# Spreading four half exponentials over the change of blocks, and moving one TensorE piece, in a graph attention kernel

## The chip, the cores and the metric

The kernel runs on one core of one Trainium2 chip, in one launch. The metric is device time in microseconds (us), lower is better; the number is the median of three runs. A core has five engines that run side by side and meet only at semaphores: TensorE (PE in the profile, its weight loads PEld), VectorE (DVE), ScalarE (ACT), GpSimd (POOL) and SyncE (SP), which issues transfers. Each engine takes its instructions strictly in the order in which they are written.

## What is computed

Two layers of a graph network over 3327 nodes with 128 features, dense adjacency matrix. Cut to what matters:

```python
# layer 0: graph attention with a mask, then residual and layer norm
e = leaky_relu(A * s + A * r.T);  att = softmax(where(A > 0, e, NEG), axis=1)
x = layernorm(x + att @ H)
# layer 1: 128 attention "heads" d, each with 8 features h, n = m = 3327
a = einsum('dnh,dmh->dnm', q, k) * scale + adj + adj
a = softmax(a, axis=2)
out = einsum('dnm,dmh->dnh', a, v).reshape(n, 1024) @ Wo.T
x = layernorm(x + out)
```

Nearly all of the time goes into layer 1: 128 x 3327 x 3327 exponentials, and the two products around them.

## The kernel before, in words

**Blocks, chunks and rounds.** Heads are taken four at a time: 32 groups `g`. The 3327 columns `n` are cut into 7 blocks of 476. For one group and one block (224 such blocks in all), the 3327 keys are walked in 26 chunks of 128 (one has 127), numbered 0 to 25. A chunk's tile `e4` holds 4 heads x 476 columns for 128 keys; a *half* is two of the four heads, 952 numbers a partition. The chunks are cut into *stretches* of three: (0,1,2), (3,4,5) and so on to (21,22,23); the last stretch has two chunks only, (24,25).

The adjacency enters in two ways. In the first chunk of each stretch (0, 3, ... 24; I call it a **product chunk**; `times` in the code) ScalarE takes the exponential of the scores straight from PSUM (L992), and GpSimd multiplies by a factor, 1 or e² (L993). In the other chunks (**sum chunks**) VectorE adds the adjacency to the scores (L995), and ScalarE takes the exponential afterwards, in place (L828, in the function `exp_late`). The exponential of a whole sum chunk is one instruction of 1904 numbers a partition.

The work is laid out in 26 *rounds* a block. Each round handles two halves. In a stretch i, i+1, i+2 the three rounds are: half of i and half of i+1; the other half of i and of i+1; both halves of i+2. The last stretch has just rounds 24 and 25. So in rounds 24, 25 and, in the next block, 0 and 1, four rounds in a row have a half of a product chunk; elsewhere every third round has none.

**The order in a round.** The loop writes, round by round: the score matmuls of the two halves (L135; four matmuls on four row groups of the array); then zero to two *pieces* of TensorE side work (`work_tensor`); then for each half L992 and L993, or L995; then `exp_late()`; then the products with the values (`products`, L800) of the chunk whose turn was four rounds ago (LAG = 4); then side work of VectorE and GpSimd (`work`). The side work is layer 0 of the rows to come and the output projection of the rows that are done: per piece one matmul such as L311, L365 or L479, and on VectorE small instructions such as L304, L284 or L374 and L377. `lane` says in which rounds there is room for it. A piece is taken only where the next unit of the side work is one for TensorE; a projection (L365), for one, is followed by a VectorE unit (L374, L377) which must be done before the next one.

**Buffers that make engines wait.** Scores of a product half go to one PSUM buffer (`pe`, one copy): the next product half's scores wait until L992 has read it. Scores of a sum half go to `pd` with two copies: they wait for the L995 of two halves ago. The products of a block pile up in one PSUM bank `av`; after the last one (written at the end of round 3 of the next block) VectorE copies it out (L809), and the first product of the next block (in round 4) waits for that copy.

**What is late.** `exp_late()` runs what the round before put on the list `late`. So chunk 23, finished in round 23, gets its whole exponential in round 24; the two halves of chunk 25 get theirs in rounds 25 and 0. In units of half a chunk ScalarE is given, in rounds 24, 25, 0, 1, 2, 3: 3, 2, 2, 1, 2, 3 units (its own L992 counted). `lane("p", n)` gives one TensorE piece in rounds 4, 7, ... 22 and 25, and two in round 24.

Of the kernel before, what the change touches and what calls it, by code (L numbers as in the profile page):

```python
# [47 lines left out]
def kernel(  # L48
# [31 lines left out]
    NT = -(-N // P)  # L80
# [7 lines left out]
    HG = 4  # L88
    NG = D // HG
# [44 lines left out]
    def scores(dst, k4, q4, i, r, j, nb, stop=True):  # L134
        nc.tensor.matmul(  # L135
            dst,
            k4[32 * j : 32 * j + H4, i::NT],
            q4[32 * j : 32 * j + H4, :nb],
            start=True,
            stop=stop,  # L140
        )


    def special():
        with ExitStack() as sx, tc.manual_schedule(engines=ALL):
# [86 lines left out]
            def tick(all_=False):  # L232
                for p in pend:
                    p[0] -= 1
                while pend and (all_ or pend[0][0] <= 0):
                    pend.pop(0)[1]()
# [471 lines left out]
            for m, st_ in enumerate(stretch):  # L708
                starts[len(rounds)] = m
                if len(st_) > 1:  # L710
                    i = st_[0]
# [5 lines left out]
            NR = len(rounds)  # L717
# [4 lines left out]
            def open_group(g):  # L722

                k4 = kp.tile([P, N], F32R, name="k4b")
                v4 = kp.tile([P, HG, VW], F32, name="v4b")
                nc.gpsimd.memset(v4[:, :, REST * H1 :], 0.0)

                def keys(j, engine=nc.sync):
                    engine.dma_start(
                        k4[32 * j : 32 * j + H4, :].bitcast(F32),  # L730
                        _ap(kT, (g * HG + j) * N, [[G, 2 * H], [0, 2], [1, N]]),
                    )

                def values(p0, p1, k, engine=nc.sync):
                    engine.dma_start(
                        v4[p0:p1, :, : k * H1],
                        _ap(vd, (g * HG * N + p0 * NT) * H1, [[NT * H1, p1 - p0], [N * H1, HG], [1, k * H1]]),
                    )

                parts = [lambda j=j, **kw: keys(j, **kw) for j in range(HG)]  # L740
                for p0, p1, k in [c + (NT,) for c in _cut(FP)] + [(FP, P, REST)]:
                    parts.append(lambda c=(p0, p1, k), **kw: values(*c, **kw))
                return k4, v4, parts
# [19 lines left out]
            def want_adj(n):  # L763

                if n >= len(stretches):
                    return
                g, b, m = stretches[n]
                a = adjs[n] = ap_.tile([P, 3, WB], F32, name="at")
                n0 = blocks[b][0]
                cs = stretch[m]  # L770
                if n >= RAW and cs[0] in times:
                    nc.sync.dma_start(a[:, 0, :], ftd[b][m])
                    cs = cs[1:]
                z = where[cs[0]]
                there = sum(i < REST for i in cs)
                parts = [(0, P, there)]
                if there < len(cs):
                    parts = [c + (len(cs),) for c in _cut(FP)] + [(FP, P, there)]
                for p0, p1, k in parts:
                    if k:  # L780
                        nc.sync.dma_start(
                            a[p0:p1, z : z + k, :],
                            _ap(adjT, (p0 * NT + cs[0]) * N + n0, [[NT * N, p1 - p0], [N, k], [1, WB]]),
                        )
# [34 lines left out]
            waiting = []  # L819


            late = []

            def exp_late():
                while late:
                    s, i, h0, h1 = late.pop(0)
                    e = s.e[i][: kr[i], h0:h1, :]
                    nc.scalar.activation(e, e, AF.Exp, scale=2.0)  # L828

# [5 lines left out]
            total = NBLK * NR  # L835
# [8 lines left out]
            def lane(kind, n):  # L844
                middle = n % 3 == 1 and 4 <= n < NR - 2
                if kind == "p":
                    return (1, 2)[n == NR - 2] if middle or n >= NR - 2 else 0
                return int(middle or n == 0 or n >= NR - 2)

            made = [layer0(t) for t in range(1, NT)]  # L850
# [3 lines left out]
            for n, (_, m, a) in enumerate(made):  # L854

                later = []
                for u in a:
                    if u[0] == "r":

                        at = max((k for k, v in enumerate(aside) if v[0] == "n"), default=0)  # L860
# [70 lines left out]
            def finish_to(mark, now):  # L931
                while mark not in marks:
                    row = "main" if head("main", -1 if now is None else now, True) else "aside"
                    if head(row, -1 if now is None else now, True) is None:
                        break
                    run(row, -1)
                    tick(True)
# [14 lines left out]
            for g in range(NG):  # L952
                k4, v4, _ = group
                for b in range(NBLK):
                    s = Block()
                    s.g, s.b, s.q4, s.k4, s.v4, s.left, s.e, added = g, b, queries[0], k4, v4, NT, {}, {}
                    for n, rnd in enumerate(rounds):
                        at = b * NR + n
                        if n in starts:
                            m = (g * NBLK + b) * NST + starts[n]  # L960
                            want_adj(m + AHEAD)
                            a = adjs[m]
                        tick()
                        if g + 1 < NG:
                            if at == total - OPEN:
                                finish_to(("rows", reads[g + 1]), None)
                                tick(True)
                                group = open_group(g + 1)
                            for k, f in enumerate(group[2]):
                                if at >= total - OPEN and at == total - OPEN + OPEN * k // len(group[2]):  # L970
                                    f()
                        if n == NR // 2 and (b + 1 < NBLK or g + 1 < NG):
                            queries = open_queries(g, b + 1) if b + 1 < NBLK else open_queries(g + 1, 0)
                        for j in range(HG):
                            if n == NR // 2 + j * (NR > 12) and (b + 1 < NBLK or g + 1 < NG):
                                queries[1](j)
                        sc = []
                        for i, h in rnd:
                            sc.append((pe if i in times else pd).tile([P, 2, 512], F32, name="scb"))
                            for t in range(2):  # L980
                                scores(sc[-1][: kr[i], t, :WB], s.k4, s.q4, i, kr[i], 2 * h + t, WB)
                        work_tensor(g * total + at, n)
                        for (i, h), z in zip(rnd, sc):
                            r = kr[i]
                            if i not in s.e:
                                s.e[i] = sp.tile([P, HG, WB], F32, name="e4")
                                added[i] = 0
                            eh = s.e[i][:r, 2 * h : 2 * h + 2, :]
                            added[i] += 1
                            ah = a[:r, where[i], :].unsqueeze(1).to_broadcast([r, 2, WB])  # L990
                            if i in times:
                                nc.scalar.activation(eh, z[:r, :, :WB], AF.Exp, scale=2.0)  # L992
                                nc.gpsimd.tensor_tensor(eh, eh, ah, op=ALU.mult)  # L993
                            else:
                                nc.vector.tensor_tensor(eh, z[:r, :, :WB], ah, op=ALU.add)  # L995
                        exp_late()
                        for i, h in rnd:
                            if i in times:
                                continue
                            if NT % 3 == 2 and i == NT - 1:  # L1000
                                late.append((s, i, 2 * h, 2 * h + 2))
                            elif added[i] == 2 and (s, i, 0, HG) not in late:
                                late.append((s, i, 0, HG))
                        if n + 1 in starts or n + 1 == NR:
                            del adjs[m]
                            make_factor(m + 1)
                        waiting.append((s, order[n]))
                        while len(waiting) > LAG:
                            products(*waiting.pop(0))
                        work(g * total + at, n)  # L1010
            exp_late()
            while waiting:
                products(*waiting.pop(0))
            tick(True)
# [378 lines left out]
```

## Time and profile before

| | us |
|---|---|
| median of three runs | 10442.8 (10442.0 to 10449.3) |
| the profiled execution's own time | 10444.2 |
| its span, first to last instruction | 10442.3 |
| L993, GpSimd's multiplications, 4032 of them | 8971.6 busy, 2.234 each |
| L995, VectorE's additions, 7616 | 8418.5 busy, 1.145 each |
| L800, products with the values, 46592 | 5874.8 busy, 0.576 each, four at a time |
| L135, score matmuls, 23296 | 4348.8 busy, 0.592 each, four at a time |
| L809, copy of a block's products, 224 | 144.3 busy, 0.644 each |

How to read it: a matmul's duration is that of one instruction, but four of them run side by side on separate parts of the array, so busy time is far below count times duration. The busy share is an average; whether an engine holds up the rest is read from what the others wait for.

Two stretches of the trace, both with one piece a stretch, in the view of busy time by window: 4875.00 to 4880.26 us, three rounds in the middle of a block, has PE busy 5.26 us, ACT 5.18, DVE 4.91, POOL 4.41 out of 5.26. Across a change of blocks, in the timeline of TensorE, the score matmuls of rounds 24, 25, 0, 1, 2, 3, 4, 5 start at 4847.95, 4850.28, 4852.39, 4854.13, 4855.60, 4857.48, 4859.20 and 4861.11 us. The rounds are therefore 2.33, 2.11, 1.74, 1.47, 1.88, 1.72 and 1.91 us long.

### The profile page before, as it was taken

Reading aid. Unit: us, or ns where it says so; the run is one execution under the profiler, and the core shown is the slowest. Engines: PE = TensorE matmul, PEld = TensorE weight load, DVE = VectorE, ACT = ScalarE, POOL = GpSimd, SP = SyncE. Lnnn points to the kernel's source line nnn. Section 1 sums busy time; section 2 is a strip of 40 time slices with the busy share of each in tenths; the row PEclk is TensorE's granted clock in tenths of the full one; section 3 lists DMA queues with packets and bytes.
Section 4 is the critical chain, followed back from the end, with each engine's and each line's share of the span. In section 5 each row is a group of like instructions: output and inputs, shape, how many; then the busy total and the mean of one; then the engine's idle time right before and its main releaser. Section 6 shows DMA issues by size and latency. Waiting matters only on the chain.

```text
span 10442.3 us, 195151 instructions
## 1 busy us (share of the span) xinstructions
PE 10174.5 (97%) x73245; PEld 3799.9 (36%) x73245; DVE 9401.7 (90%) x12247; ACT 10077.8 (97%) x8087; POOL 9229.0 (88%) x4395
## 2 busy tenths in 40 slices
PE   7999999999999999999999999999999999999998
PEld 3333333333333333333333333333333333333333
DVE  6999999999989999989999998999999899998887
ACT  6999999999999999999999999999999999999998
POOL 6988898889888889888889888888888888888887
PEclk8999999999999999999999999999999999999999
DMA  6655555555555555555555555555555555555554
GB/s 174 200 169 165 167 166 171 166 169 159 173 159 169 166 161 167 173 163 171 153 169 169 166 175 164 157 163 175 171 164 164 159 169 172 165 155 165 162 156 123
DMA packets 1176730, 1728.91 MB, mean 166 GB/s; under 512 B 121852, under 2 KB 1164381, under 8 KB 1171547
## 3 DMA queue, kind: packets, MB, share of 16 engines
q1 hardware_dynamic: 1174410, 1714.80, 55.0%
q8 instruction: 576, 9.44, 0.4%
q14 instruction: 383, 3.14, 0.1%
q10 hardware_dynamic: 1361, 1.53, 0.1%
HBM read 1611.92 MB, written 103.95 MB: 164 GB/s over the span
## 4 chain that ended last, share of the span: by engine, by line
PE 79%; ACT 13%; DVE 3%; issue 2%; POOL 2%; DMA 1%; SPq 0%; DVEq 0%; ACTq 0%; POOLq 0%
PE av L800 40%; PE scb L135 33%; ACT e L992 7%; ACT e L828 6%; PE bank L311 2%; PE bank L365 2%; DVE e L995 2%; POOL e L993 1%; PE bank L479 1%; DVE o L809 0%; DMA at<-in_adjT_dram 0%; POOL at L790 0%; PE bank L460 0%; DMA trow<-td 0%; DVE lo L377 0%
## 5 line engine op out<-in xcount | busy, mean ns | idle before, releaser
L993 POOL TENSOR_TENSOR e<-e,at 128x952 f32<-128x952 f32 x4032 | 8971.6, 2234 | 1099.2 <-ACT e L992 911.1
L995 DVE TENSOR_TENSOR e<-scb,at 128x952 f32<-128x952 f32 (+1 forms) x7616 | 8418.5, 1145 | 914.4 <-PE scb L135 651.8
L828 ACT ACTIVATE e<-e 128x1904 f32<-128x1904 f32 (+1 forms) x4032 | 6856.9, 1701 | 79.0 <-DVE e L995 77.2
L800 PE MATMUL av<-e,v4b 128*32 128x476 f32 x46592 | 5874.8, 576 | 28.9 <-DVE o L809 19.2
L135 PE MATMUL scb<-q4b,k4b 32*128 32x476 f32 (+1 forms) x23296 | 4348.8, 592 | 180.6 <-ACT e L992 99.0
L135 PEld LDWEIGHTS scb<-q4b,k4b 32*128 32x128 f32 (+1 forms) x23296 | 2390.9, 295 | 5002.8 <-issue 1984.9
L992 ACT ACTIVATE e<-scb 128x952 f32<-128x952 f32 x4032 | 3873.8, 961 | 203.0 <-PE scb L135 103.1
L800 PEld LDWEIGHTS av<-e,v4b 128*32 128x32 f32 x46592 | 919.4, 108 | 1216.6 <-issue 810.6
L311 PE MATMUL bank<-hsb,w 128*128 128x129 f32 (+2 forms) x1300 | 300.7, 321 | 0.0
L304 DVE TENSOR_SCALAR_CACHE_REDUCE dump<-a 128x384 bf16<-128x384 f32 (+2 forms) x468 | 247.4, 529 | 0.6
L284 DVE TENSOR_SCALAR_CACHE_REDUCE w<-trow,er 128x128 f32<-128x128 f32 (+1 forms) x650 | 221.1, 340 | 20.6 <-DMA trow<-td 12.6
L311 PEld LDWEIGHTS bank<-hsb,w 128*128 128x128 f32 (+2 forms) x1300 | 188.6, 188 | 133.5 <-issue 133.5
L295 POOL TENSOR_TENSOR w<-w,a 128x384 f32<-128x384 f32 (+3 forms) x225 | 221.6, 985 | 0.1
L809 DVE COPY o<-av 128x476 f32<-128x476 f32 x224 | 144.3, 644 | 5.5 <-PE av L800 5.5
L377 DVE SCALAR_TENSOR_TENSOR lo<-bank,hi 128x128 fp32r<-128x128 f32 (+1 forms) x400 | 116.7, 292 | 13.9
L374 DVE TENSOR_SCALAR hi<-bank 128x128 fp32r<-128x128 f32 (+1 forms) x400 | 112.5, 281 | 0.0
L365 PE MATMUL bank<-wv,x1T 128*128 128x128 f32 (+1 forms) x400 | 98.2, 328 | 4.8 <-DVE vb L396 4.3
L365 PE MATMUL bank<-wk,x1T 128*128 128x128 f32 (+1 forms) x400 | 97.6, 326 | 3.7 <-DVE lo L377 3.2
L365 PE MATMUL bank<-wq,x1T 128*128 128x128 f32 (+1 forms) x400 | 97.7, 326 | 2.9 <-DVE lo L377 1.9
L479 PE MATMUL bank<-wo,ot 128*128 128x128 f32 (+1 forms) x416 | 95.9, 325 | 0.4 <-DVE ot L469 0.4
L365 PEld LDWEIGHTS bank<-wv,x1T 128*128 128x128 f32 (+1 forms) x400 | 59.8, 188 | 51.4 <-issue 39.9
L365 PEld LDWEIGHTS bank<-wk,x1T 128*128 128x128 f32 (+1 forms) x400 | 59.5, 187 | 50.9 <-issue 40.3
(111 smaller groups left out, 824.9 us busy)
## 6 DMA issues: line engine op xcount, KB each, us to landing
at<-in_adjT_dram SPq DMA_DIRECT2D x1736, 476.0 KB
at<-ftd SPq DMA_DIRECT2D x1953, 238.0 KB
q4b<-qT SPq DMA_DIRECT2D x1788, 29.8 KB
k4b<-kT SPq DMA_DIRECT2D x126, 415.9 KB
at<-in_adjT_dram SPq DMA_DIRECT2D x217, 208.2 KB
at<-in_adjT_dram SPq DMA_DIRECT2D x56, 714.0 KB
a<-in_adjT_dram SPq DMA_DIRECT2D x50, 504.0 KB
ftd<-at SPq DMA_DIRECT2D x63, 238.0 KB
```

The source lines that it names most:

```text
L135: nc.tensor.matmul(dst, k4[32 * j : 32 * j + H4, i::NT], q4[32 * j : 32 * j + H4, :nb], start=True, stop=stop,)
L284: nc.vector.tensor_scalar(w, s["t"][:, :r], e, None, op0=ALU.max, op1=ALU.add, accum_out=spare[:, 0:1])
L295: nc.gpsimd.tensor_tensor(w, w, s["a"][n][:, c0 - i0 : c1 - i0, :r], op=ALU.mult)
L304: nc.vector.tensor_scalar(z, a, float(k), None, op0=ALU.is_equal, op1=ALU.add, accum_out=even[:, t, at : at + 1])
L311: nc.tensor.matmul(s["p"][:r, : D + 1], s["w"][i // CW][: kr[i], i % CW, :r], hsb[: kr[i], i, :], start=(i == 0), stop=(i == NT - 1),)
L365: nc.tensor.matmul(s["b"][:r, :QW], s["xT"][:, :r], w[:, c : c + QW], start=True, stop=True)
L479: nc.tensor.matmul(s["b"][:r, :D], s["ot"][:, h, :r], wo[:, h, :], start=(h == 0), stop=(h == H - 1))
L800: nc.tensor.matmul(s.av[32 * j : 32 * j + 32, :], s.v4[:r, j, i * H1 : i * H1 + 32], e[:r, j, :], start=(s.left == NT - 1), stop=(s.left = ...
L828: nc.scalar.activation(e, e, AF.Exp, scale=2.0)
L992: nc.scalar.activation(eh, z[:r, :, :WB], AF.Exp, scale=2.0)
L993: nc.gpsimd.tensor_tensor(eh, eh, ah, op=ALU.mult)
L995: nc.vector.tensor_tensor(eh, z[:r, :, :WB], ah, op=ALU.add)
```

## The change

The list `late` gets a due round for each entry. A whole sum chunk is due one round after its second half, as before. Chunk 23 (`NT - 3`) is now taken in two halves, due in rounds 24 and 25. Chunk 25 (`NT - 1`) is still in halves, each now due two rounds after its addition, in rounds 0 and 1 of the next block. ScalarE's units in rounds 24, 25, 0, 1, 2, 3 are then 2, 2, 2, 2, 2, 3. In `lane`, round 24 has room for one TensorE piece in place of two, and round 3 for one in place of none.

```diff
-            def exp_late():
-                while late:
-                    s, i, h0, h1 = late.pop(0)
+            def exp_late(now):
+                for item in [x for x in late if x[0] <= now]:
+                    late.remove(item)
+                    _, s, i, h0, h1 = item
                     e = s.e[i][: kr[i], h0:h1, :]
                     nc.scalar.activation(e, e, AF.Exp, scale=2.0)
...
                 if kind == "p":
-                    return (1, 2)[n == NR - 2] if middle or n >= NR - 2 else 0
+                    return int(middle or n == 3 or n >= NR - 2)
...
-                        exp_late()
+                        now = g * total + at
+                        exp_late(now)
                         for i, h in rnd:
                             if i in times:
                                 continue
                             if NT % 3 == 2 and i == NT - 1:
-                                late.append((s, i, 2 * h, 2 * h + 2))
-                            elif added[i] == 2 and (s, i, 0, HG) not in late:
-                                late.append((s, i, 0, HG))
+                                late.append((now + 2, s, i, 2 * h, 2 * h + 2))
+                            elif NT % 3 == 2 and i == NT - 3:
+                                late.append((now + 1 + h, s, i, 2 * h, 2 * h + 2))
+                            elif added[i] == 2 and (now + 1, s, i, 0, HG) not in late:
+                                late.append((now + 1, s, i, 0, HG))
...
-            exp_late()
+            exp_late(NG * total + 2)
```

## The prediction

> **What bounds the kernel now.** I read the page first: engine shares, the chain, the groups.
>
> ```profile
> PE 10174.5 (97%) x73245; PEld 3799.9 (36%) x73245; DVE 9401.7 (90%) x12247; ACT 10077.8 (97%) x8087; POOL 9229.0 (88%) x4395
> ...
> PE 79%; ACT 13%; DVE 3%; issue 2%; POOL 2%; DMA 1%; SPq 0%; DVEq 0%; ACTq 0%; POOLq 0%
> ...
> L828 ACT ACTIVATE e<-e 128x1904 f32<-128x1904 f32 (+1 forms) x4032 | 6856.9, 1701 | 79.0 <-DVE e L995 77.2
> ...
> L992 ACT ACTIVATE e<-scb 128x952 f32<-128x952 f32 x4032 | 3873.8, 961 | 203.0 <-PE scb L135 103.1
> ```
>
> TensorE and ScalarE are both 97% busy, and the chain runs 79% through TensorE, 13% through ScalarE. Neither has more than 3% to give, so the change can only win stalls at the change of blocks. The window view finds no TensorE idle in a middle stretch with a piece (5.26 of 5.26 us); middle stretches without one last 5.07 us in the TensorE timeline. Next I read the timeline at two changes of blocks. Time 0 is from here the start of round 24's scores. First ScalarE, at a change with no TensorE piece (0 = 4940.19):
>
> ```profile
> 4941.75 1.78 ACT L828 ACTIVATE e<-e 128x1904 f32<-128x1904 f32 x1
> 4943.43 0.96 ACT L992 ACTIVATE e<-scb 128x952 f32<-128x952 f32 x1
> 4944.28 1.00 ACT L828 ACTIVATE e<-e 127x952 f32<-127x952 f32 x1
> 4945.21 0.96 ACT L992 ACTIVATE e<-scb 128x952 f32<-128x952 f32 x1
> 4946.07 0.99 ACT L828 ACTIVATE e<-e 127x952 f32<-127x952 f32 x1
> 4946.96 0.96 ACT L992 ACTIVATE e<-scb 128x952 f32<-128x952 f32 x1
> 4948.51 1.79 ACT L828 ACTIVATE e<-e 128x1904 f32<-128x1904 f32 x1 [0.59 <-DVE e L995]
> 4950.36 0.96 ACT L992 ACTIVATE e<-scb 128x952 f32<-128x952 f32 x1
> ```
>
> Chunk 23's whole exponential (1.78) stands ahead of round 25's L992; round 0's scores need that L992's buffer and start at 4944.44. Then ScalarE runs dry (0.59, and again before 4950.36). This is a real stall. Now TensorE at a change with projections in rounds 24 and 25 (0 = 4847.95):
>
> ```profile
> 4854.13 0.60 PE L135 MATMUL scb<-q4b,k4b 32*128 32x476 f32 x4 [0.20 <-ACT e L992]
> 4854.66 1.01 PE L800 MATMUL av<-e,v4b 128*32 128x476 f32 x8
> 4855.60 1.02 PE L135 MATMUL scb<-q4b,k4b 32*128 32x476 f32 x4
> 4856.55 1.00 PE L800 MATMUL av<-e,v4b 127*32 127x476 f32 x8
> 4857.48 0.62 PE L135 MATMUL scb<-q4b,k4b 32*128 32x476 f32 x4
> 4858.04 1.00 PE L800 MATMUL av<-e,v4b 128*32 128x476 f32 x8
> ```
>
> The product of chunk 25 is the one at 4856.55 (127 rows), at +8.60; what it needs of ScalarE had ended at 4854.96. Here the stall on ScalarE before 4854.13 is small.
>
> **Hand-over times, from these rows.** Scores to their L992 or L995: 0.70. L992: 0.96, next start after 0.86. Half L828: 0.99, next after 0.89 (4946.07 to 4946.96). Whole L828: 1.79, next after 1.69. End of L992 to the next product half's scores: 0.05. So two product rounds in a row are at least 0.70 + 0.96 + 0.05 = 1.71 apart. On TensorE scores take 0.53 of the queue, products 0.94, a piece 0.42 (4848.93 to 4849.35). L995: 1.15. Three L995 (3.26 together) lead from round 2's scores to the copy L809, which starts 5.36 after round 1's scores (4859.48).
>
> From round 24 to round 7 the trace's changes take 16.54 (median) where both rounds 24 and 25 have a piece, and 16.39 otherwise. Rounds 5 to 7 keep their 3.38 after the change, so I only have to follow the first product of the new block (round 4).
>
> **Part by part.** The written order of the TensorE instructions gives the pieces of rounds 24 and 25 over 222 changes. Both rounds: 137 before, 149 after; neither: 28 and 42.
>
> *Gain: a half in front of L992 instead of a whole chunk.* Without a piece, L992 of round 25 starts at 1.56 + 0.89 = 2.45 instead of 3.24; round 0's scores at 3.46 instead of 4.25; its L992 at 3.31 + 0.89 = 4.20; round 1's scores at 5.21 instead of 6.03. VectorE's side units in rounds 24, 25 and 0 (about 0.5 each) leave some 0.75 of this 0.82. ScalarE is then without a gap, GpSimd has its 2.23 multiplications in rows of 6.6 and follows. 32 changes have no piece in round 3 either: 32 x -0.75 = -24. Ten have pieces in rounds 3 and 4, which take part back: 10 x -0.39 = -4. A piece in one round only: 18 x -0.28 and 7 x -0.25 = -7; six more come out at zero.
>
> *Nothing gained behind projections.* 68 changes have projections in both rounds. Round 25's waits for VectorE's L377 of round 24's, so round 0 starts at 4.44 in both kernels; round 1 at 6.15 instead of 6.17.
>
> *New wait: chunk 25's second half.* Its exponential was behind round 0's L992 and is now behind round 1's. In the written order the third of the four product instructions of chunk 25, in round 2, waits for it, and everything of TensorE queues behind. ScalarE: L992 of round 1 starts after the half before it, at 5.14 + 0.86 + 0.89 = 6.89, the half at 7.75, it ends at 8.74; product at 8.79 instead of 8.60. So round 3 starts 0.20 later. Trace of before has no such wait; its price is bounded by 0 (the first two heads fill the time) and by these 0.20.
>
> *The moved piece.* In round 3 it stands ahead of the block's last product. Cover is VectorE, which without it copies at 11.53 only: with the piece the product starts at 9.73 + 0.53 + 0.42 = 10.68, ends at 11.68, the copy starts 0.06 later, at 11.74. The piece in round 4, which before stood in the wait for the copy, is gone in these 68; the first product of the new block is late by 0.20: 68 x 0.20 = +14. Where the cover is gone, the piece costs its whole 0.42.
>
> *Pieces of the other kind, 81 changes.* Round 24 loses its second piece: round 0 starts at 4.21 instead of 4.44, round 1 at 5.93 instead of 6.18. The new wait puts the product at 8.56 and round 3 at 9.50, as before (9.52). With pieces in rounds 3 and 4 (69) the new block's first product comes at 9.50 + 1.89 + 0.95 = 12.34 instead of 12.23: 69 x 0.11 = +8. The 12 without them win 0.25: -3.
>
> *Twelve more changes with pieces in both rounds*, at 0.15: +2. The sum: -24 - 4 - 7 + 14 + 8 - 3 + 2 = **-14**, say -15 with rounding. The split adds 224 instructions to ScalarE, each 2 x 0.89 - 1.69 = 0.09 by starts, 20 us in all, already in the chain above where ScalarE is the path. No DMA and nothing of SP's or POOL's queue changes place.
>
> The two halves are dearer by another book: the Trainium skill, "ScalarE: Activation LUTs", section "Rules for kernel authors", budgets about 0.3 us for each activation plus 0.83 ns for each element. By that the split would cost 224 x 0.3 = 67 us of ScalarE, an estimate that would make the change slower; the rows (1.79 whole, 0.99 half, next after 0.89) show most of a start hidden behind the instruction before.
>
> **Forecast.** 10444.2 (profiled execution; the median is 1.4 below) - 15 = **10429**, the middle of what counts as no change here: about 0.2% (21 us) is what a measurement of this kernel tells from none.
>
> **Rivals.** *The new wait does not bind* (0.30): the first two heads' products run meanwhile, and the half lands in time. Then round 3 comes 0.20 earlier in about 137 changes, -27: 10402. For it: two of the four product instructions are free to go. Against: they run side by side with the other two (8 in 1.00 us), so they save nothing. *ScalarE only moves its backlog* (0.18), ending slower: in changes without pieces it has no gap in the rounds that follow; if its lag at round 7 (L992 1.45 after the scores) grows by what round 1 gained, the gains of 24 + 4 + 7 are gone, and the 73 changes concerned pay the split's 0.09, +7: 10444 - 15 + 35 + 7 = 10471. It decides from a lag above about 2.3 (3.35 to the next product scores, less 0.96 and 0.05). Against: both ScalarE and the TensorE-VectorE loop have 5.07 there, so the lag should stand. *Nothing happens* (part of my 0.52): gains and waits cancel, 10444.
>
> Chances: forecast 0.52, as "same"; faster 0.30; slower 0.18. The range takes in both outer cases: 10398 to 10472.
>
> **What would show it.** Idle before L992 and L828 from L995 falls; a new wait of products (L800) on ScalarE of about 0.2 appears in some 137 changes; rounds 0 and 1 start earlier only where pieces are missing; the copy L809 starts to wait for products. If products show no wait on ScalarE, or the middle stretches lengthen, I am wrong.

## The result, and the profile after

The changed kernel takes **10421.05 us** (median of six runs, 10419.71 to 10424.65) against 10442.88 of the kernel before (six runs beside it, 10441.99 to 10449.3): ratio 0.9978, 95% interval 0.9965 to 0.9991. It is faster by 22 us, where 15 were forecast. The profiled execution spans 10418.4 us (before: 10442.3).

These are the lines of the page of the changed kernel that answer to those shown of before. L830 is now the late exponential, L994 the exponential of a product chunk, L995 GpSimd's multiplication, L997 VectorE's addition; L135, L800 and L809 keep their numbers. Behind them stand the rows of before for L800 and L809.

```profile
PE 10195.1 (98%) x73245; PEld 3823.1 (37%) x73245; DVE 9410.9 (90%) x12247; ACT 10088.8 (97%) x8311; POOL 9223.5 (89%) x4395
...
PE 84%; ACT 8%; DVE 4%; issue 1%; DMA 1%; POOL 1%; SPq 0%; DVEq 0%; ACTq 0%; POOLq 0%
...
L830 ACT ACTIVATE e<-e 128x1904 f32<-128x1904 f32 (+2 forms) x4256 | 6875.3, 1621 | 17.5 <-DVE e L997 16.4
L800 PE MATMUL av<-e,v4b 128*32 128x476 f32 x46592 | 5905.4, 575 | 37.6 <-DVE o L809 30.7
...
L994 ACT ACTIVATE e<-scb 128x952 f32<-128x952 f32 x4032 | 3871.4, 960 | 228.9 <-PE scb L135 133.7
...
L809 DVE COPY o<-av 128x476 f32<-128x476 f32 x224 | 145.9, 651 | 27.6 <-PE av L800 6.8
```

```profile
L800 PE MATMUL av<-e,v4b 128*32 128x476 f32 x46592 | 5874.8, 576 | 28.9 <-DVE o L809 19.2
...
L809 DVE COPY o<-av 128x476 f32<-128x476 f32 x224 | 144.3, 644 | 5.5 <-PE av L800 5.5
```

Read the right-hand part first. ScalarE's idle time ahead of the late exponential, 79.0 us before, is 17.5; ahead of L994 it rose by 26, from 203.0 to 228.9. The chain's share of ScalarE fell from 13% to 8%. VectorE now waits 27.6 us ahead of the copy L809, 5.5 before; 20.8 of it are 160 gaps of some 0.13 us, and the row names a releaser only for the four longer ones. One thing is easy to miss: the products L800 are *busy* 5905.4 us, 30.6 more than before, with the same instructions.

Next the timeline of ScalarE in the changed kernel, at a change of blocks with no TensorE piece in rounds 24, 25, 3 and 4 (0 = 4610.84; columns: start, duration, then the instruction):

```profile
4611.54 0.97 ACT L994 ACTIVATE e<-scb 128x952 f32<-128x952 f32 x1
4612.40 0.99 ACT L830 ACTIVATE e<-e 128x952 f32<-128x952 f32 x1
4613.29 0.96 ACT L994 ACTIVATE e<-scb 128x952 f32<-128x952 f32 x1
4614.13 1.00 ACT L830 ACTIVATE e<-e 128x952 f32<-128x952 f32 x1
4615.06 0.96 ACT L994 ACTIVATE e<-scb 128x952 f32<-128x952 f32 x1
4615.92 0.99 ACT L830 ACTIVATE e<-e 127x952 f32<-127x952 f32 x1
4616.81 0.95 ACT L994 ACTIVATE e<-scb 128x952 f32<-128x952 f32 x1
4617.65 2.68 ACT L830 ACTIVATE e<-e 127x952 f32<-127x952 f32 x2
```

One half exponential after each L994, with no gap. Round 25's L994 starts at 2.45, as predicted (3.24 before). Chunk 25's second half comes behind round 1's L994: it is the first of the two instructions merged in the last line, a half and the whole exponential of the next sum chunk.

What that does to TensorE is seen in its timeline at a change with projections in rounds 24 and 25 (0 = 4931.87):

```profile
4938.04 0.61 PE L135 MATMUL scb<-q4b,k4b 32*128 32x476 f32 x4 [0.20 <-ACT e L994]
4938.57 1.01 PE L800 MATMUL av<-e,v4b 128*32 128x476 f32 x8
4939.51 1.02 PE L135 MATMUL scb<-q4b,k4b 32*128 32x476 f32 x4
4940.46 1.19 PE L800 MATMUL av<-e,v4b 127*32 127x476 f32 x8
4941.59 0.60 PE L135 MATMUL scb<-q4b,k4b 32*128 32x476 f32 x4
```

The group with 127 rows is the product of chunk 25. It takes 1.19 instead of 1.00: its first two heads start, the other two stand until the second half is ready (its exponential ends at 4940.61, their matmuls start at 4940.66). No idle time is recorded, since TensorE is busy with the first two. That is the new wait, and L800's longer busy time comes from it: in the trace 204 of 220 such groups take over 1.1 us, 1.21 in the median; 2 did before. The wait alone adds 41 us, as "half first" will show: without it L800 is busy 10 us less than before, so that 30.6 are left.

From round 24 to round 7, over 220 changes (those into blocks 3 to 222, counted from 1), the sum of the TensorE timelines went from 3644.3 to 3618.9 us: -25.4. The rest of the blocks, rounds 7 to 24, went from 6480.0 to 6482.7, and the first score starts 1.8 later. These three make -20.9 of the span's -23.9; the other 3 lie in the first two and the last two blocks.

### The profile page after: what moved, and what is told of

Same layout as the page of the kernel before. It is cut to its first block, busy times and chain, and to the rows that moved or that the text cites. A ratio compares the mean times of both kernels' runs of the same rounds, so it can differ in the third digit from the quotient of the medians.

```text
span 10418.4 us, 195134 instructions
## 1 busy us (share of the span) xinstructions
PE 10195.1 (98%) x73245; PEld 3823.1 (37%) x73245; DVE 9410.9 (90%) x12247; ACT 10088.8 (97%) x8311; POOL 9223.5 (89%) x4395
## 4 chain that ended last, share of the span: by engine, by line
PE 84%; ACT 8%; DVE 4%; issue 1%; DMA 1%; POOL 1%; SPq 0%; DVEq 0%; ACTq 0%; POOLq 0%
PE av L800 44%; PE scb L135 34%; ACT e L994 5%; ACT e L830 3%; PE bank L311 3%; DVE e L997 2%; PE bank L365 2%; POOL e L995 1%; PE bank L479 1%; DVE o L809 1%; DMA at<-in_adjT_dram 0%; PE bank L460 0%; DVE ot L469 0%; DMA k4b<-kT 0%; DVE lo L377 0%
## 5 line engine op out<-in xcount | busy, mean ns | idle before, releaser
L995 POOL TENSOR_TENSOR e<-e,at 128x952 f32<-128x952 f32 x4032 | 8966.3, 2234 | 1078.4 <-ACT e L994 903.2
L997 DVE TENSOR_TENSOR e<-scb,at 128x952 f32<-128x952 f32 (+1 forms) x7616 | 8417.6, 1144 | 857.5 <-PE scb L135 639.1
L830 ACT ACTIVATE e<-e 128x1904 f32<-128x1904 f32 (+2 forms) x4256 | 6875.3, 1621 | 17.5 <-DVE e L997 16.4
L800 PE MATMUL av<-e,v4b 128*32 128x476 f32 x46592 | 5905.4, 575 | 37.6 <-DVE o L809 30.7
L135 PE MATMUL scb<-q4b,k4b 32*128 32x476 f32 (+1 forms) x23296 | 4339.0, 592 | 124.5 <-ACT e L994 62.3
L135 PEld LDWEIGHTS scb<-q4b,k4b 32*128 32x128 f32 (+1 forms) x23296 | 2378.4, 296 | 4925.1 <-issue 1936.8
L994 ACT ACTIVATE e<-scb 128x952 f32<-128x952 f32 x4032 | 3871.4, 960 | 228.9 <-PE scb L135 133.7
L800 PEld LDWEIGHTS av<-e,v4b 128*32 128x32 f32 x46592 | 948.3, 108 | 1223.1 <-issue 770.1
L809 DVE COPY o<-av 128x476 f32<-128x476 f32 x224 | 145.9, 651 | 27.6 <-PE av L800 6.8
L479 PEld LDWEIGHTS bank<-wo,ot 128*128 128x128 f32 (+1 forms) x416 | 63.0, 193 | 46.1 <-issue 45.5
```

Source lines behind the costliest of these rows:

```text
L135: nc.tensor.matmul(dst, k4[32 * j : 32 * j + H4, i::NT], q4[32 * j : 32 * j + H4, :nb], start=True, stop=stop,)
L479: nc.tensor.matmul(s["b"][:r, :D], s["ot"][:, h, :r], wo[:, h, :], start=(h == 0), stop=(h == H - 1))
L800: nc.tensor.matmul(s.av[32 * j : 32 * j + 32, :], s.v4[:r, j, i * H1 : i * H1 + 32], e[:r, j, :], start=(s.left == NT - 1), stop=(s.left = ...
L809: nc.vector.tensor_copy(o4, s.av)
```

## The experiments

Each kernel's median stands beside that of before measured along with it, with the 95% interval of their ratio; then the two sums, in us, from the profiled execution.

| kernel | median | before | interval of the ratio | rounds 24 to 7 | rounds 7 to 24 |
|---|---|---|---|---|---|
| before | | | | 3644.3 | 6480.0 |
| after | 10421.05 | 10442.88 | 0.9965 to 0.9991 | 3618.9 | 6482.7 |
| exponentials only | 10422.84 | 10443.69 | 0.9971 to 0.9989 | 3624.6 | 6479.3 |
| piece only | 10452.03 | 10443.69 | 0.9999 to 1.0017 | 3649.6 | 6481.1 |
| scores twice | 10439.39 | 10443.69 | 0.9987 to 1.0005 | 3634.5 | 6480.6 |
| half first | 10394.57 | 10443.69 | 0.9939 to 0.9966 | 3592.6 | 6481.9 |
| only chunk 25 late | 10479.17 | 10443.24 | 1.0021 to 1.0046 | 3677.9 | 6480.9 |
| only chunk 23 split | 10546.17 | 10443.24 | 1.0082 to 1.0113 | 3750.1 | 6480.8 |
| half first, piece in round 8 | 10406.79 | 10443.24 | 0.9952 to 0.9979 | 3576.3 | 6510.8 |
| after, piece in round 8 | 10422.20 | 10443.24 | 0.9972 to 0.9990 | 3591.6 | 6511.6 |

My theory was the prediction's, with one addition that the first comparison called for: where a stall was long, TensorE's clock fell after it, and that goes too. The rivals were "the new wait does not bind" and "ScalarE only moves its backlog".

### Exponentials only

The changed kernel with `lane` as before:

```diff
-                    return int(middle or n == 3 or n >= NR - 2)
+                    return (1, 2)[n == NR - 2] if middle or n >= NR - 2 else 0
```

> The exponentials spread as in the changed kernel, TensorE's pieces as before (two in round 24, none in round 3). My theory (ScalarE's stall goes where pieces are missing, a new wait of 0.2 us in round 2 comes, and the TensorE clock no longer halves at the changes of blocks): changes without pieces win 0.6 us each, 123 changes with pieces in rounds 24, 25 and 4 lose 0.17, some 9 us come from the clock, whose half-speed stretches after the start fall from 9 to 1 or 2; together about -13 us against before, 10430. Rival (the moved piece brought the gain): as before, 10443, within 5.

Measured 10422.84. Against before that is nearly the whole of the change; against after it is 1.8 more, inside the scatter of either. The exponentials alone make the gain. It is 7 us better than expected. The expectation's terms, 27 x -0.6, -9 and 123 x 0.17, make -4 and not its -13; in the traces the changes without pieces won 24.5 us, about as expected, those with a piece in one of rounds 24 and 25, for which it has no term, won 10, and those with pieces in both lost 15, not 21.

### Piece only

The kernel before with the changed kernel's `lane`:

```diff
-                    return (1, 2)[n == NR - 2] if middle or n >= NR - 2 else 0
+                    return int(middle or n == 3 or n >= NR - 2)
```

> Only the piece moved (one in round 24, one in round 3), exponentials as before. My theory: ScalarE still holds round 0 at 4.25 us and round 1 at 6.03, the moved piece is hidden behind VectorE's additions, so nothing is won: 10443, between -3 and +6; the clock still halves at 6 to 10 changes of blocks. Rival (the moved piece brought the gain): 10425.

Measured 10452.03, 8 more than before, 2 beyond the range expected, with 1 just inside the interval. Moved alone, the piece brings no gain, and if anything a small loss: in changes without pieces, 41 instead of 27, round 0 still starts at 4.25 and round 1 at 6.03. TensorE waits there for ScalarE, so taking a piece out of round 24 brings nothing.

### Scores twice

The kernel before, and where rounds 24 and 25 have no piece, round 25's four score matmuls are issued a second time, into the same buffer (`took` and `took24` count the pieces of rounds 25 and 24). This keeps the exponentials as they were and only gives TensorE something to do in the gap.

```diff
...
+                        if n == NR - 1 and took + took24 == 0:
+                            for (i, h), z in zip(rnd, sc):
+                                for t in range(2):
+                                    scores(z[: kr[i], t, :WB], s.k4, s.q4, i, kr[i], 2 * h + t, WB)
```

> The kernel before, but in round 25 of the changes that have no piece in rounds 24 and 25 the four score matmuls are issued a second time (same values into the same buffers): TensorE's gap of about 0.9 us before round 0 shrinks to about 0.35, and ScalarE's order is that of before. Theory of the clock (the half-speed stretches follow from TensorE's gaps): most of the 9 half-speed stretches at changes of blocks vanish, 10434, -6 to -10. Rival (the clock falls for another reason, such as position in time): stretches stay, 10443 or some us more for the added work.

What it is to tell is in the window view of **before**. Its columns are the window, its length, the busy time of PE, PEld, DVE, ACT and POOL (with the number of instructions), the granted clock, the DMA share and GB/s. The first two windows are at the change of blocks that begins at 9578.49, the other two at the one that begins at 4435.85; neither has pieces.

```profile
9580.08:9583.49 3.41, 2.29 (x20) 0.98 (x24) 1.65 (x2) 3.41 (x4) 2.95 (x2) 1.00 0.71 209
9583.49:9586.90 3.41, 3.41 (x20) 0.55 (x18) 2.13 (x2) 2.83 (x4) 3.41 (x2) 0.50 0.24 61
```

```profile
4436.21:4439.62 3.41, 2.75 (x24) 0.62 (x20) 3.41 (x6) 3.41 (x4) 3.07 (x2) 1.00 0.41 110
4439.62:4443.04 3.42, 2.79 (x24) 1.02 (x24) 2.42 (x6) 3.42 (x5) 3.18 (x3) 1.00 0.32 117
```

In the first pair a window holds the whole gap of 0.99 us and a small one; TensorE is busy for 2.29 of 3.41. In the next window its granted clock is 0.50, and that change takes 17.65 us from round 24 to 7. In the second pair the same gap is cut in two, 2.75 and 2.79 are busy, the clock stays at 1.00, and the change takes 16.39.

With the gap filled, the half-clock stretches between 120 and 10380 us fell from 11 to 2, and those 27 changes from 16.87 to 16.52 on average, 9.5 us in all, though round 0 starts at 4.25 as before. The span fell by 7.7 (first score 1.6 later). The median fell by 4.3 only, less than the 6 to 10 expected, and its interval holds 1. So the trace shows the effect; the clock alone does not show a gain in time that the runs can tell from none.

### Half first

The changed kernel with chunk 25's second half written ahead of round 1's L994, not behind it:

```diff
+                        if n == 1:
+                            exp_late(g * total + at)
                         for (i, h), z in zip(rnd, sc):
```

> The changed kernel, but chunk 25's second half exponential stands ahead of round 1's L994 (L992 before) in ScalarE's queue, not behind it. Theory of the new wait (product of chunk 25 waits 0.2 us for it in about 137 changes): the wait goes, round 3 starts 0.2 earlier there, and the first product of the new block as well: -28 us against the changed kernel, 10393. Rival (the wait costs nothing since the copy waits for VectorE anyway): as the changed kernel, 10421.

Measured **10394.57**: 49 less than before and 26 less than after, the best of all versions. The page's line and the same place in TensorE's timeline, at a change with a piece in round 24 only:

```profile
L800 PE MATMUL av<-e,v4b 128*32 128x476 f32 x46592 | 5864.4, 575 | 43.2 <-DVE o L809 34.6
```

```profile
4836.65 1.00 PE L135 MATMUL scb<-q4b,k4b 32*128 32x476 f32 x4
4837.59 1.00 PE L800 MATMUL av<-e,v4b 127*32 127x476 f32 x8
4838.52 0.65 PE L135 MATMUL scb<-q4b,k4b 32*128 32x476 f32 x4
```

The product of chunk 25 takes 1.00 again, none of the 220 over 1.1 us, and L800 is busy 41 us less than in after. Changes with pieces in rounds 24, 25 and 3, but not in 4, take 16.58 in place of 16.75 (medians). The wait is worth 26 us of time, and "the new wait does not bind" falls.

### Only chunk 25 late

The changed kernel without the two halves of chunk 23:

```diff
-                            elif NT % 3 == 2 and i == NT - 3:
-                                late.append((now + 1 + h, s, i, 2 * h, 2 * h + 2))
```

> The changed kernel with chunk 23's exponential whole again, in round 24; chunk 25's halves stay late, pieces as in the changed kernel. My theory: ScalarE again holds round 0 at 4.25 us where pieces are missing, round 1 comes at 5.97 instead of 5.24 there, so about 42 changes lose 0.6 us and 30 lose 0.2; where both rounds have pieces nothing changes (round 1 at 5.95 to 6.16); a few half-speed stretches of the TensorE clock come back: +32 to +40, 10457. Rival (splitting chunk 23 only costs ScalarE's 20 us): faster than the changed kernel, 10405.

Measured 10479.17, worse than before by 36 and than expected by 22. ScalarE at a change without pieces (0 = 4635.13):

```profile
4636.69 1.79 ACT L830 ACTIVATE e<-e 128x1904 f32<-128x1904 f32 x1
4638.37 0.96 ACT L994 ACTIVATE e<-scb 128x952 f32<-128x952 f32 x1
4640.14 0.96 ACT L994 ACTIVATE e<-scb 128x952 f32<-128x952 f32 x1 [0.81 <-PE scb L135]
```

Chunk 23's whole exponential stands ahead of round 25's L994 again (3.24), and round 0's L994 finds ScalarE empty, with nothing to put there. The gain is gone, the new wait has stayed. I had the stall's price too low: round 1 starts at 6.03 (expected 5.97), and there are ten half-clock stretches. The traces tell where the 22 us lie. Against the changed kernel, changes without pieces lost 36 us (0.6 x 42 = 25 expected); 8 of these are clock, since eight such changes touched by a half-clock stretch take 17.48 on average and the others 16.51. Those with a piece in one round lost 10 (6 expected). Those with pieces in both rounds lost 12, where none was expected: behind pieces that are not projections ScalarE holds round 0 at 4.25 instead of 4.21 and round 1 at 6.03 instead of 5.95.

### Only chunk 23 split

The changed kernel with chunk 25's halves due as before:

```diff
-                                late.append((now + 2, s, i, 2 * h, 2 * h + 2))
+                                late.append((now + 1, s, i, 2 * h, 2 * h + 2))
```

> The changed kernel with chunk 25's halves one round earlier, as before; chunk 23 in two halves. My theory: the second half of 23 then stands with the first of 25 ahead of round 0's L994, which starts at 5.66 instead of 5.14 or less after a gap in round 24, so round 1 comes at 6.67 instead of 5.95 to 6.16 in changes with pieces and at 6.10 instead of 5.24 without: 0.3 to 0.9 us at every change, +115 against the changed kernel, 10535. The wait of chunk 25's product on ScalarE is gone all the same. Rival (the new wait is the whole cost, and splitting 23 the whole gain): 10393.

Measured 10546.17, 103 more than before. The timelines at a change without pieces (0 = 4664.20), ScalarE and then TensorE:

```profile
4667.49 1.88 ACT L830 ACTIVATE e<-e 128x952 f32<-128x952 f32 x2
4669.26 0.96 ACT L994 ACTIVATE e<-scb 128x952 f32<-128x952 f32 x1
```

```profile
4668.43 1.01 PE L800 MATMUL av<-e,v4b 128*32 128x476 f32 x8
4670.28 0.60 PE L135 MATMUL scb<-q4b,k4b 32*128 32x476 f32 x4 [0.84 <-ACT e L994]
```

Two halves, of chunks 23 and 25, now stand together ahead of round 0's L994: the block of 1.8 us has only moved on by a round. Round 1 pays, at 6.08, and with pieces, where it had been at 6.17, at 6.60. So the stall reaches the changes that had none, and there are 21 half-clock stretches. Neither half of the exponentials' change is worth anything without the other.

### A piece in round 8 in place of round 3

Once with "half first", once with the changed kernel:

```diff
-                    return int(middle or n == 3 or n >= NR - 2)
+                    return int(middle or n == 8 or n >= NR - 2)
```

> The run with chunk 25's second half first, and the moved piece in round 8 instead of round 3. My theory: in round 8 the piece fills the 0.43 us in which round 9's second scores wait for VectorE's addition, so it costs nearly nothing, while in round 3 it makes the copy wait (0.05 us behind projections, 0.16 with pieces in rounds 3 and 4): -13 against that run, 10382. Rival (a TensorE piece costs its 0.42 wherever TensorE is busy): +40 or more, 10435.

> The changed kernel with the moved piece in round 8 instead of round 3 and nothing else. My theory: the new wait of chunk 25's product stays (0.2 us), the copy no longer waits for the piece: -0.07 us at 71 changes and -0.16 at 60, 10407. Rival (piece costs its 0.42 in round 8): 10460.

Measured 10406.79 and 10422.20: both miss, 25 and 15 above what was expected. The table tells where: the change of blocks won 16.3 and 27.3 us, where 13 and 15 were expected, and rounds 7 to 24 gave back 28.9 each. TensorE's timeline of the second kernel, rounds 7 to 10:

```profile
4950.81 0.60 PE L135 MATMUL scb<-q4b,k4b 32*128 32x476 f32 x4
4951.34 0.49 PE L365 MATMUL bank<-wv,x1T 128*128 128x128 f32 x2
...
4952.69 0.61 PE L135 MATMUL scb<-q4b,k4b 32*128 32x476 f32 x4
4953.23 0.49 PE L311 MATMUL bank<-hsb,w 128*128 128x129 f32 x2
...
4954.58 0.62 PE L135 MATMUL scb<-q4b,k4b 32*128 32x476 f32 x4
...
4956.29 0.60 PE L135 MATMUL scb<-q4b,k4b 32*128 32x476 f32 x4 [0.15 <-ACT e L994]
```

Round 8 grows from 1.47 to 1.89 and round 9 gets shorter, from 1.90 to 1.71, but not by the piece's whole 0.42: between two product rounds the scores wait for L994 (0.15 here), the floor of 1.71 that the prediction itself had worked out. A stretch takes 5.07 without a piece, 5.26 with one and 5.49 with two. I had not applied the floor to the middle of the block.

## Why the prediction was right, and where it was not

The forecast was built of medians by kind of change. Over the 220 changes, with the means that the traces show (a change counts as "both" if rounds 24 and 25 each have a piece):

| kind | before: count, taken as, measured | after: count, predicted, measured |
|---|---|---|
| both | 136, 16.54, 16.56 | 148, 16.67, 16.63 |
| neither | 27, 16.39, 16.87 | 41, 15.73, 15.82 |
| one | 57, 16.39, 16.43 | 31, 16.17, 16.42 |
| sum | 3626.2, 3644.3 | 3613.4, 3618.9 |

The predicted means are the prediction's terms divided by its counts: -24 and -4 over 42 changes without pieces; +14, +8 and -3 over 149 with both; 18 x -0.28 and 7 x -0.25 over 31 with one.

- **The gain without pieces: right in mechanism, its size too small.** Rounds 25 and 0 came where I put them (L994 at 2.45, round 0 at 3.46), round 1 at 5.24 (5.21). By medians the change went from 16.41 to 15.84; away from half clock the means fell by 0.62, where 0.66 had been forecast. What I left out is in the "before" column: I took 16.39 for changes that cost 16.87 on average. The excess, 27 x 0.48 = 13 us, comes from nine changes that a half-clock stretch touches; they take 17.77, the other eighteen 16.42. Six of the nine follow straight on the stall (7 us of the 13); one, at 10084.18, has a wait of 1.71 for VectorE of its own. In the changed kernel the stall is gone and with it these stretches: three are left in place of 11, all before 390 us. So the sum before was 18.1 higher than I had taken it and the sum after only 5.5 higher: the change of blocks won 25.4 in place of 12.8. In the changed kernel a miss is hidden: the kind "one" came out 31 x 0.25 = 8 us dearer than forecast, and the kind "both" 6 us cheaper. One reading was too strong: the second time that ScalarE was to run dry, before 4950.36, is a gap of 0.06 us.
- **Nothing behind projections: right.** Round 0 at 4.43, round 1 at 6.17 in the changed kernel (4.44 and 6.15 predicted).
- **The new wait: right in mechanism, its count too low.** Round 3 at 9.71 instead of 9.51 behind projections, the 0.20 forecast, and "half first" puts a price of 26 us on it; the prediction's 0.20 in about 137 changes is 27. That the two agree is partly luck. The wait came in 204 changes, in 25 of the 41 without pieces too; without it round 3 starts 38.6 us earlier over the 220 changes, and by round 7 a third of that is gone. And the sign I had named, products waiting for ScalarE, would have misled: the profile's list of waits has none, it is in the longer groups only.
- **The moved piece: right.** The copy now waits for products, 27.6 us ahead of L809, and only when both are there, the late product and the piece in round 3: 6.9 in "half first", 6.3 in "exponentials only". Behind projections the changes take 16.76, predicted 16.74; most of that rise is the new wait, since without the moved piece ("exponentials only") they take 16.69.
- **Pieces of the other kind: right,** 16.65 (predicted 16.65) with pieces in 3 and 4, 16.32 (16.29) without; of the first there are 60, not 69.
- **"ScalarE only moves its backlog": falls.** Rounds 7 to 24 grew by 2.7 us, not by 35.
- **The price of a split.** The Trainium skill, "ScalarE: Activation LUTs", "Rules for kernel authors", budgets about 0.3 us for an activation whose bias is a pointer operand; from that came the prediction's estimate of 67 us for 224 more. The rows decide, and show less: 2 x 0.99 - 1.79 = 0.19 us of fixed part each, of which about half lies behind the instruction before (0.09 by starts). The late exponentials' busy time rose from 6856.9 to 6875.3, 18.4 us or 0.08 each.

The range held the time; but I gave "faster" 0.30 and "same" 0.52, and the runs show faster by 0.21%, on the edge between the two. The term that was mis-sized is the price of a change without pieces in the kernel before: 16.39 in the sum, 16.87 in the trace. With the six changes' 7 us of half clock priced, the forecast would have been 10422; that this lies so near to 10421 is partly luck, since the other misses, several us each, happen to cancel.

## What to carry to other kernels

When late work is spread over an engine's strict order, ask who waits for each part: here the half that a product needs stood behind an exponential that nobody was waiting for, and swapping the two was worth more than the whole change. A wait inside a group of instructions that run side by side shows as a longer busy time (here 1.21 in place of 1.00 us), not as idle time, so compare busy time and group lengths too. A price taken from undisturbed medians leaves out what a stall does afterwards; check means against medians by kind, and look up the floors before calling a place free.

## What the hardware showed that was not expected

The half clock follows a fixed grid. In the kernel before the stretches start at 159.3, 384.6, 712.3, 1729.4, 2831.9, 9583.5 and so on; their distances are whole multiples of 3.4133 us (66, 162, 460, 783, 2761 of them from the first), and each lasts 3.41 or twice that. Counting TensorE's busy share by the windows of this grid that run at full clock, from 460 to 10385 us in all ten traces, a half-clock window never followed one over 0.77 busy; at 0.72 to 0.77 it followed in 8 of 152, at 0.65 to 0.71 in 32 of 90, at 0.61 or less in 10 of 11. In the three kernels that keep the gap ahead of round 0 (before, piece only, only chunk 25 late), 65 such gaps are 0.86 to 1.00 us long. Where one lay whole in a window with another gap of about 0.1 us or more, half clock followed in 16 of 26; whole and alone, in 2 of 21; cut by a border, in 2 of 18. That is why only some of the changes without pieces were slow. Between 0.65 and 0.77 the busy share does not decide alone; what does is not shown. Nor does every stretch stem from that gap: in three of the nine changes that one touched in the kernel before, it began ahead of the gap or followed another wait.

The Trainium skill, "TensorE: Matmul & The Clock Gate", in "What's actually happening", has a free-running window of 3413 ns, and the grid agrees. It gives half rate after at least one idle window; here a window with 2.29 of 3.41 us busy was enough.
